# A two-layer graph network on one core: where five pieces of work stand, and which engine and queue they use

## The chip, the core and the metric

The kernel runs on one core of a Trainium2 chip. A core has five engines with a queue of instructions each: TensorE (PE in the profile, with PEld for its loads of weights), VectorE (DVE), ScalarE (ACT), GpSimd (POOL) and SyncE (SP). Each works through its queue in order and waits on semaphores for the others. Transfers are issued from the queues of SP, POOL and ScalarE and run on 16 DMA engines. The metric is the time of one execution on the device in microseconds, smaller being better; it is given as the median of several executions.

## The reference

x holds 128 graphs of 128 nodes with 256 features, adj their adjacency. Both layers begin with a normalization over the features and a relu, and add their result to x. Cut to what matters:

```python
# layer 0
h = relu(layernorm(x))
xc   = transpose(h)                                   # features by nodes
c    = bn2(conv17(relu(bn1(conv1(xc)))))              # 1x1, then 17 taps along the nodes
x_conv = transpose(relu(c + xc))
s    = h @ w_se.T + b_se                              # embedding of 3 numbers per node
A    = exp(-squared_distances(s)) * adj
x_nmp = A @ relu(h @ w_msg.T + b_msg)
r, z, n = GRU gates of (concat(x_conv, x_nmp), h)     # sigmoid, sigmoid, tanh
x = x + (1 - z) * n + z * h
# layer 1: only nodes 0 to 24 change
h = relu(layernorm(x))
for g, idx in enumerate(GROUPS):                      # five sets of 25, 9, 7, 6, 6 nodes
    a = normalized(adj[:, idx][:, :, idx] + I)
    o = relu(a @ relu(a @ h[:, idx] @ W1[g] + b1[g]) @ W2[g] + b2[g])
    fused[:, idx] += softmax(fusion_w)[g] * o
x = x + fused
```

Everything is float32.

## The kernel before

The graphs are taken in 32 groups of four (`q`). The 17-tap convolution is done by Fourier products: a forward transform of each half of a graph (80 points), one product per frequency, and an inverse transform. The 32 groups form two batches of 16 for this.

The program has these stages:

- **Stage A** (`stage_a`, one per group) loads x (`load_x`, four pieces on SP's queue, L360), takes the moments (`moments`: L267, L268, L269 on VectorE, then `rs` on POOL, L270), scales (`normalize`, L275), transposes (`ph`, L387), applies the relu into `hTa` (L389) and stores it to device memory (`hTd`, POOL, L392), multiplies with the 1x1 convolution (`pc`, L398), and transforms (`pf`, L409) into `X` (L415, L417). Four buffers hold x, two hold `hTa`.
- **`tap_weights`** runs beside stage A of the first batch. It loads the taps (`wt`), transforms them (`pw`, L451) through three staging buffers `ws`, and stores them (`wfd`, POOL, L463). At a certain step it calls `load_late`, which loads `wse` (L252) and the later part of the constants `cst` (L253) on SP's queue. At its end it opens the pools in which the neighbour stage works.
- **Stage B** (`stage_b`, once per batch) makes the 40 frequency products: `load_w` loads the transformed taps three steps ahead (`wf`, L488), `add` forms sums on POOL, PE makes `pa` and `pb` (L502), VectorE and ScalarE evacuate them into `y` (L524, L525), and POOL stores `y` to `yd` (L529).
- **`early`** (one per group) is the neighbour stage: it loads `hT` and `adj` (L540, L542), makes the embedding `pse` (L581), four scalings of it into `ef` (two on VectorE, L586, two on ScalarE, L589), their products `lr` (L592), the messages (`pm`, L601, and L604, L606), the distances `pd` (L614), exp times adjacency `aT` (L618, L619), and `px` (L627), stored on POOL's queue (`xmd`).
- **`fold_gates`** loads the gate weights and forms sums of them on POOL (L323); it runs in the second batch.
- **Stages N and C** load what the earlier ones stored and make the inverse transform (`pi`, L674), the gates (`p`, L709) and the new x (`po`, L855).
- **Layer 1** runs beside stage C: `setup_1` (loads, and the softmax of `fusion_w` with its product `s2w`, L895 to L907), `rows`, `prepare` and `block`, the last once per 16 graphs. A block ends with four quarters of four graphs, each with three steps: `turn` transposes (L1062, copied at L1066), `gather` multiplies with the adjacency (L1074, L1076, L1077), and `fuse` adds the groups together and onto x (L1083, L1085). Then four stores of x to `out` follow on POOL's queue (L1094).

The order of the instructions is fixed when the program is built. Each stage is a generator whose `yield a, b` says how much of PE's time its step takes and how long its result takes to come; `Lane` and `Order` interleave these programs on a planned clock. A batch runs its stage A with `beside` (taps, then neighbour groups) until stage A is done, then stage B with `beside`:

```python
begin = Lane([stage_a(q) for q in range(bat * BQ, (bat + 1) * BQ)], ahead=3)
order.run(begin, beside, *[gates] * bat, until=begin)
...
order.run(products, beside, *[gates] * bat, until=products)
```

So a step that is moved changes what the planner puts after it. Buffers of the on-chip memory are given out by pools; where a pool takes over the place of a closed one, a tile waits for the tiles that lay there before.

Of the kernel before, what the change touches and what calls it, by code (L numbers as in the profile page):

```python
# [9 lines left out]
FP = mybir.dt.float32  # L10
AF = mybir.ActivationFunctionType
# [196 lines left out]
def kernel(ctx: ExitStack, tc: tile.TileContext, x, adj, consts, vecs, w_se, conv1_w,  # L208
# [41 lines left out]
    def load_late():  # L250

        nc.sync.dma_start(out=wse, in_=w_se.rearrange("(k p) o -> p k o", p=P))  # L252
        nc.sync.dma_start(out=cst[:, CFIRST:], in_=consts[:, CFIRST:])  # L253

    scl, sft = {}, {}
# [84 lines left out]


# [26 lines left out]
    def stage_a(q):  # L368
# [6 lines left out]
        if q not in MOM:  # L375
            MOM[q] = moments(XA[q], "a")
            yield 0.0, 3.0
            normalize(XA[q], XA[q], *MOM[q])
            yield 0.0, 2.0
# [56 lines left out]
    def tap_weights():  # L436

        yield 0.0, 16.0
        for n in range(4):
            for m in range(8):  # L440
                if m == (0 if n else 3) and n < 3:
                    load_taps(n + 1, nc.sync, nc.gpsimd)
                if (n, m) == (2, 4):
                    load_late()
                if m % 2 == 0:
                    ws = tw.tile([P, 4, 4, D], FP, tag="ws", name=f"ws{n}_{m}", bufs=3)
                pws = [(pgat if r < 3 else ptmp).tile([P, 2, D], FP, tag="gat" if r < 3 else "tmp",
                                                      name=f"pw{n}_{m}_{r}") for r in range(4)]
                for r in range(4):
                    rows = slice(32 * r, 32 * r + TAPS)  # L450
                    nc.tensor.matmul(pws[r][:F], c("tap")[rows], wts[n][rows, 2 * m:2 * m + 2],  # L451
                                     start=True, stop=True)
                i = m % 2 * 2
                for r in range(4):
                    if r < 2 or (r == 2 and m % 2):
                        nc.scalar.activation(ws[:F, r, i:i + 2], pws[r][:F], AF.Copy)
                    else:
                        nc.vector.tensor_copy(ws[:F, r, i:i + 2], pws[r][:F])
                yield 0.9, 2.2
                if m % 2:  # L460
                    for r in range(4):
                        i0 = 64 * r + 16 * n + 2 * (m - 1)
                        nc.gpsimd.dma_start(out=wfd[:, i0:i0 + 4], in_=ws[:F, r])  # L463
# [6 lines left out]
        LATE["io"] = near.enter_context(tc.tile_pool(name="io", bufs=2, reuse_waits="tile"))  # L470
        LATE["fr"] = near.enter_context(tc.tile_pool(name="fr", bufs=1, reuse_waits="tile"))
# [6 lines left out]
    def stage_b(bat):  # L478
# [29 lines left out]
        for f in range(NF + 1):  # L508
            if f + 3 <= NF:
                load_w(f + 3)  # L510
            if f < NF:
                add(f + 1)
            y = xf.tile([P, 2, D], FP, tag="y", name=f"y{bat}_{f}")
# [61 lines left out]
    def neighbours(q, hT, ad, xm):  # L575
# [8 lines left out]
        for i in range(4):  # L584
            if i % 2 == 0:
                nc.vector.tensor_scalar(ef[:, i], pse[:, :N], emb[:, i:i + 1], embb[:, i:i + 1],  # L586
                                        op0=ALU.mult, op1=ALU.add)
            else:
                nc.scalar.activation(ef[:, i], pse[:, :N], AF.Identity, scale=emb[:, i:i + 1],  # L589
                                     bias=embb[:, i:i + 1])  # L590
# [280 lines left out]
    def setup_1():  # L871
# [9 lines left out]
        fus = pool.tile([P, NG], FP, name="fus")  # L881
        nc.sync.dma_start(out=fus, in_=fusion_w.partition_broadcast(P))
# [10 lines left out]

        fmx = pool.tile([P, 1], FP, name="fmx")
        nc.vector.reduce_max(fmx, fus, axis=mybir.AxisListType.X)  # L895
        nc.vector.tensor_scalar(fus, fus, fmx, None, op0=ALU.subtract)  # L896
        nc.scalar.activation(fus, fus, AF.Exp)
        fsm = pool.tile([P, 1], FP, name="fsm")
        nc.vector.reduce_sum(fsm, fus, axis=mybir.AxisListType.X)
        nc.vector.reciprocal(fsm, fsm)  # L900
        nc.vector.tensor_scalar(fus, fus, fsm, None, op0=ALU.mult)
        nc.vector.tensor_mul(fus, fus, c("grp"))
        wrow = pool.tile([P, 1], FP, name="wrow")
        nc.vector.reduce_sum(wrow, fus, axis=mybir.AxisListType.X)
        s2w = S["s2w"] = pool.tile([P, 2 * WIDE], FP, name="s2w")
        nc.vector.tensor_scalar(s2w, c("s2"), wrow, None, op0=ALU.mult)
# [95 lines left out]
    def block(blk):  # L1002
        while not (blk in P_DONE and blk - 1 in B1_DONE):
            yield 0.0, 0.5
        pool, yz, b2row, s2w = S["pool"], S["yz"], S["b2row"], S["s2w"]
# [51 lines left out]
        def turn(q):  # L1057
# [7 lines left out]
            zt = zts[q] = pool.tile([P, 2, D], FP, tag="zt", name=f"zt{blk}_{q}", bufs=3)  # L1065
# [13 lines left out]
        def fuse(q):  # L1079
# [5 lines left out]
            nc.vector.tensor_add(x1[:, q], x1[:, q], pf)  # L1085

        for what, q in ((turn, 0), (turn, 1), (turn, 2), (gather, 0), (gather, 1), (fuse, 0),
                        (turn, 3), (gather, 2), (fuse, 1), (gather, 3), (fuse, 2), (fuse, 3)):
# [4 lines left out]
        for j in range(GB):  # L1093
            nc.gpsimd.dma_start(  # L1094
                out=out[blk * SB:(blk + 1) * SB, :WIDE].rearrange("(q j) n c -> j n q c", j=GB)[j],
                in_=x1[j * WIDE:(j + 1) * WIDE])
# [11 lines left out]
    gates = Lane([fold_gates()], weight=0.5)  # L1108
# [61 lines left out]
```

## Time and profile before

| | us |
|---|---|
| median of 3 executions | 2099.61 |
| lowest, highest | 2089.95, 2099.69 |
| the profiled execution: its own time | 2107.02 |
| the profiled execution: span from the first to the last instruction | 2105.2 |
| PE busy in the span | 2045.2 |
| DVE, ACT, POOL busy | 1181.8, 686.8, 725.5 |
| mean granted TensorE clock | 0.986 |

The stages of the profiled execution lie in time as follows: stage A of the first batch to about 178 us, stage B to 372, stage A of the second batch to about 535, its stage B to 706, then stages N and C with layer 1 beside them to about 2015, and the last block of layer 1 to the end.

A wait is written as engine, tile and line, an arrow, and who released it; then the sum, the count and the longest in us. A window's row gives the stretch and its length, the busy time of each engine with its count of instructions, the granted clock, the share of the DMA engines' time and the rate. A timeline's row gives start, length, engine, line, operation and tiles, and in brackets the idle time before and its releaser. Letters after an engine's name: a q (SPq, POOLq) is its sequencer, which issues and waits.

### The profile page before, as it was taken

The page shows a single profiled execution, that of the slowest core. Times are in us where ns is not written, and L with a number is a line of the kernel's source. Part 1 is how long each engine was busy: PE and PEld are TensorE (multiplying, and loading weights), DVE is VectorE, ACT ScalarE, POOL GpSimd, SP SyncE. Part 2 cuts the span into 40 slices and gives each one's busy share as a digit, 9 for nine tenths or more (in the row PEclk, how much of TensorE's full clock was granted, in tenths as well). Part 3 has the DMA queues.
Part 4 walks back from the last instruction along what each step waited for, and adds up shares of the span by engine and source line. Part 5 has one row for each costly group of instructions (what it writes and reads, how often), then busy time and mean ns, then how long its engine had stood idle before and what let it go on. Part 6 is the DMA issues. An engine that isn't in the chain of part 4 may idle for free.

```text
span 2105.2 us, 31050 instructions
## 1 busy us (share of the span) xinstructions
PE 2045.2 (97%) x11316; PEld 1657.3 (79%) x11316; DVE 1181.8 (56%) x2775; ACT 686.8 (33%) x1543; POOL 725.5 (34%) x902
## 2 busy tenths in 40 slices
PE   7978999999999999999999999999999999999998
PEld 5656888789888788787878877878787787878875
DVE  6754544786544455655654565565565655654642
ACT  4643222344222333323232232232233223223333
POOL 3432666232565222503322233224323323233230
PEclk9989999999999999999999999999999999999999
DMA  9977778744777634222323332323232333223121
GB/s 217 276 227 231 240 266 264 211 153 143 250 258 257 210 111 141 75 78 73 89 71 92 87 83 72 88 71 91 75 96 73 79 91 93 78 81 98 31 79 51
DMA packets 186870, 281.67 MB, mean 134 GB/s; under 512 B 20745, under 2 KB 139982, under 8 KB 186718
## 3 DMA queue, kind: packets, MB, share of 16 engines
q1 hardware_dynamic: 156270, 185.00, 31.0%
q0 software_dynamic: 30160, 94.46, 14.1%
q8 instruction: 90, 1.47, 0.3%
q14 instruction: 62, 0.51, 0.1%
q10 hardware_dynamic: 288, 0.22, 0.0%
HBM read 187.34 MB, written 92.27 MB: 133 GB/s over the span
## 4 chain that ended last, share of the span: by engine, by line
PE 91%; DMA 4%; DVE 2%; issue 1%; POOL 1%; ACT 0%; SPq 0%; POOLq 0%; DVEq 0%; ACTq 0%
PE p L709 41%; PE pa L502 7%; PE pm L601 5%; PE ph L1031 5%; PE pz L1040 5%; PE pc L398 4%; PE pb L502 3%; PE pi L674 3%; PE px L627 3%; PE pf L409 2%; PE pg L1074 1%; PE ph L387 1%; PE pc L688 1%; PE po L855 1%; DMA xa<-in_x 1%; PE py L1014 1%
## 5 line engine op out<-in xcount | busy, mean ns | idle before, releaser
L835 POOL TENSOR_TENSOR d<-hTc,r 128x512 f32<-128x512 f32 x64 | 81.3, 1271 | 370.9 <-ACT r L832 370.9
L502 PE MATMUL pa<-wf,X 128*128 128x256 f32 x640 | 152.5, 381 | 0.0
L864 POOL DMA_DIRECT2D out<-xt x128 | 71.9, 567 | 211.0 <-DVE xt L861 205.4
L525 DVE SCALAR_TENSOR_TENSOR y<-pa,kk 128x512 f32<-128x512 f32 x78 | 53.8, 690 | 147.0 <-ACT kk L524 147.0
L398 PE MATMUL pc<-c1w,hTa 128*128 128x256 f32 x512 | 125.4, 392 | 6.6 <-DVE X L415 4.3
L709 PE MATMUL p<-th,wrz 128*128 128x256 f32 x512 | 131.7, 380 | 0.0
L724 ACT ACTIVATE z<-z,brz 128x256 f32<-128x256 f32 x128 | 58.1, 501 | 225.5 <-DVE z L781 191.2
L709 PE MATMUL p<-tc,wrz 128*128 128x256 f32 x512 | 131.6, 380 | 0.0
L709 PE MATMUL p<-tm,wrz 128*128 128x256 f32 x512 | 131.5, 380 | 0.0
L502 PEld LDWEIGHTS pa<-wf,X 128*128 128x128 f32 x640 | 118.3, 190 | 16.2 <-issue 2.2
L601 PE MATMUL pm<-wmsg,hT 128*128 128x256 f32 x512 | 124.4, 389 | 0.0
L691 DVE SCALAR_TENSOR_TENSOR xc<-pc,s_bn,hTc 128x256 f32<-128x256 f32 x128 | 53.1, 478 | 118.3 <-PE pc L688 118.3
L398 PEld LDWEIGHTS pc<-c1w,hTa 128*128 128x128 f32 x512 | 96.0, 195 | 25.9 <-DVE X L415 4.5
L601 PEld LDWEIGHTS pm<-wmsg,hT 128*128 128x128 f32 x512 | 97.9, 194 | 16.7 <-issue 1.8
L1031 PE MATMUL ph<-yz,w 128*128 128x96 f32 (+3 forms) x640 | 109.2, 325 | 0.9 <-DVE yz L1016 0.9
L1033 ACT ACTIVATE hh<-ph,vec 128x96 f32<-128x96 f32 (+3 forms) x160 | 64.0, 402 | 134.2 <-PE ph L1031 124.7
L709 PEld LDWEIGHTS p<-tm,wrz 128*128 128x128 f32 x512 | 97.5, 190 | 13.0
L1040 PE MATMUL pz<-hh,w 128*128 128x96 f32 (+3 forms) x640 | 107.3, 322 | 0.0
L1031 PEld LDWEIGHTS ph<-yz,w 128*128 128x128 f32 x640 | 88.1, 193 | 21.9 <-issue 13.2
L709 PEld LDWEIGHTS p<-tc,wrz 128*128 128x128 f32 x512 | 95.2, 190 | 12.0 <-issue 0.5
L709 PEld LDWEIGHTS p<-th,wrz 128*128 128x128 f32 x512 | 94.9, 190 | 12.1 <-DVE fus L896 0.3
L709 PE MATMUL p<-hTc,wrz 128*128 128x256 f32 x384 | 103.9, 394 | 0.0
(204 smaller groups left out, 4562.0 us busy)
## 6 DMA issues: line engine op xcount, KB each, us to landing
wf<-wfd SPq DMA_DIRECT2D x160, 256.0 KB, 4.1
wfd<-ws POOLq DMA_DIRECT2D x64, 320.0 KB, 8.2
yd<-y POOLq DMA_DIRECT2D x80, 256.0 KB, 3.8
yt<-yd SPq DMA_DIRECT2D x64, 320.0 KB, 4.9
w<-in_W SPq DMA_DIRECT2D x40, 512.0 KB, 3.7
xa<-in_x SPq DMA_DIRECT2D x128, 128.0 KB, 5.2
hTd<-hTa POOLq DMA_DIRECT2D x32, 512.0 KB, 5.8
hT<-hTd SPq DMA_DIRECT2D x32, 512.0 KB
```

The lines of the kernel that those rows point to most:

```text
L398: nc.tensor.matmul(pc[:, i], hT[:, k, (2 * h + i) * N:(2 * h + i + 1) * N], c1w[:, k], start=(k == 0), stop=(k == 1))
L502: nc.tensor.matmul(ps, xk(k), WF[f][:, k, s], start=(k == 0), stop=(k == 1))
L601: nc.tensor.matmul(pm[:, i], hT[:, k, j * N:(j + 1) * N], LATE["wmsg"][:, k], start=(k == 0), stop=(k == 1))
L627: nc.tensor.matmul(px[:, dc, i], msgs[h][:, i, dc * P:(dc + 1) * P], aT[:, 2 * h + i], start=True, stop=True)
L674: nc.tensor.matmul(pi[b * 64:(b + 1) * 64], inv[:F], yt[:, b::2], start=True, stop=True)
L709: nc.tensor.matmul(ps[:, m], w[:, i, k, m * P:(m + 1) * P], factor(i, x, t), start=first and j == 0, stop=last and j == len(n) - 1, skip_g ...
L724: nc.scalar.activation(dst[:, m], src[:, m], AF.Sigmoid, bias=brz[:, b + m:b + m + 1])
L835: nc.gpsimd.tensor_sub(d, hT[:, dc], r[:, dc])
L864: nc.gpsimd.dma_start(out=out[q * GB + j, WIDE:].rearrange("(t n) c -> n t c", n=WIDE), in_=xt[j * WIDE:(j + 1) * WIDE, 1:4])
L1031: nc.tensor.matmul(ph, w1[:, k, m * P:(m + 1) * P], yz[:, k, :, o:o + n], start=(k == 0), stop=(k == 1))
L1033: nc.scalar.activation(hh[:, m], ph, AF.Relu, bias=v("b1", g * 4 + m))
L1040: nc.tensor.matmul(pz, w2[:, g, m, cc * P:(cc + 1) * P], hs[g][:, m], start=(m == 0), stop=(m == 3))
```

## The change

Five edits are made together.

1. The load of `fusion_w` (`fus`) moves from `setup_1` into `load_late`, and `load_late` is called at step (1, 3) of `tap_weights` instead of (2, 4).
2. The softmax of `fusion_w` moves from `setup_1` into a program of its own, `fold_fusion`, which follows `fold_gates` in the same lane; `fus` and `s2w` lie in the pool of constants.
3. Stage B of the first batch loads x of groups 16, 17 and 18 in its steps 33, 36 and 39 into a new pool `xe`, which is opened ahead of the pool `fr`; it takes the moments of group 16 in step 36 and scales it in step 38. In stage A, groups 17 and 18 wait 1 and 12 us of the planned clock before their moments.
4. All four scalings `ef` are made by ScalarE.
5. The last steps of a block stand in another order, with four buffers `zt` in place of three. Each quarter is stored as soon as it is fused: one store on POOL's queue for blocks 0 to 6; for block 7 four stores, on SP's queue, those of the last quarter in turn on SP's and ScalarE's.

```diff
     def load_late():
 
+        nc.sync.dma_start(out=fus, in_=fusion_w.partition_broadcast(P))
         nc.sync.dma_start(out=wse, in_=w_se.rearrange("(k p) o -> p k o", p=P))
         nc.sync.dma_start(out=cst[:, CFIRST:], in_=consts[:, CFIRST:])
 
+    fus = cp.tile([P, NG], FP, name="fus")
+    s2w = cp.tile([P, 2 * WIDE], FP, name="s2w")
...
+    def fold_fusion():
+
+        fmx = cp.tile([P, 1], FP, name="fmx")
+        nc.vector.reduce_max(fmx, fus, axis=mybir.AxisListType.X)
+        nc.vector.tensor_scalar(fus, fus, fmx, None, op0=ALU.subtract)
+        nc.scalar.activation(fus, fus, AF.Exp)
+        yield 0.0, 4.0
+        fsm = cp.tile([P, 1], FP, name="fsm")
+        nc.vector.reduce_sum(fsm, fus, axis=mybir.AxisListType.X)
+        nc.vector.reciprocal(fsm, fsm)
+        nc.vector.tensor_scalar(fus, fus, fsm, None, op0=ALU.mult)
+        yield 0.0, 4.0
+        nc.vector.tensor_mul(fus, fus, c("grp"))
+        wrow = cp.tile([P, 1], FP, name="wrow")
+        nc.vector.reduce_sum(wrow, fus, axis=mybir.AxisListType.X)
+        nc.vector.tensor_scalar(s2w, c("s2"), wrow, None, op0=ALU.mult)
+        yield 0.0, 0.0
...
         if q not in MOM:
+            if BQ < q < BQ + 3:
+                yield 0.0, 11.0 * (q - BQ) - 10.0
             MOM[q] = moments(XA[q], "a")
...
-                if (n, m) == (2, 4):
+                if (n, m) == (1, 3):
                     load_late()
...
         LATE["io"] = near.enter_context(tc.tile_pool(name="io", bufs=2, reuse_waits="tile"))
+        LATE["xe"] = near.enter_context(tc.tile_pool(name="xe", bufs=1, reuse_waits="tile"))
         LATE["fr"] = near.enter_context(tc.tile_pool(name="fr", bufs=1, reuse_waits="tile"))
...
             if f < NF:
                 add(f + 1)
+            if f >= NF - 6 and f % 3 == 0 and bat + 1 < NBAT:
+                n = (bat + 1) * BQ + (f - NF + 6) // 3
+                XA[n] = LATE["xe"].tile([P, 4, D], FP, name=f"xa{n}")
+                load_x(XA[n], n)
+            n = (bat + 1) * BQ
+            if f == NF - 3 and n in XA:
+                MOM[n] = moments(XA[n], "a")
+            if f == NF - 1 and n in XA:
+                normalize(XA[n], XA[n], *MOM[n])
...
         for i in range(4):
-            if i % 2 == 0:
-                nc.vector.tensor_scalar(ef[:, i], pse[:, :N], emb[:, i:i + 1], embb[:, i:i + 1],
-                                        op0=ALU.mult, op1=ALU.add)
-            else:
-                nc.scalar.activation(ef[:, i], pse[:, :N], AF.Identity, scale=emb[:, i:i + 1],
-                                     bias=embb[:, i:i + 1])
+            nc.scalar.activation(ef[:, i], pse[:, :N], AF.Identity, scale=emb[:, i:i + 1],
+                                 bias=embb[:, i:i + 1])
...
-            zt = zts[q] = pool.tile([P, 2, D], FP, tag="zt", name=f"zt{blk}_{q}", bufs=3)
+            zt = zts[q] = pool.tile([P, 2, D], FP, tag="zt", name=f"zt{blk}_{q}", bufs=4)
...
             nc.vector.tensor_add(x1[:, q], x1[:, q], pf)
-
-        for what, q in ((turn, 0), (turn, 1), (turn, 2), (gather, 0), (gather, 1), (fuse, 0),
-                        (turn, 3), (gather, 2), (fuse, 1), (gather, 3), (fuse, 2), (fuse, 3)):
+            b0 = blk * SB + q * GB
+            if blk < NBLK - 1:
+                nc.gpsimd.dma_start(out=out[b0:b0 + GB, :WIDE], in_=x1[:, q])
+                return
+            for j in range(GB):
+                eng = nc.scalar if q == QS - 1 and j % 2 else nc.sync
+                eng.dma_start(out=out[b0 + j, :WIDE], in_=x1[j * WIDE:(j + 1) * WIDE, q])
+
+        for what, q in ((turn, 0), (turn, 1), (turn, 2), (gather, 0), (turn, 3), (gather, 1),
+                        (gather, 2), (fuse, 0), (gather, 3), (fuse, 1), (fuse, 2), (fuse, 3)):
             what(q)
...
-        for j in range(GB):
-            nc.gpsimd.dma_start(
-                out=out[blk * SB:(blk + 1) * SB, :WIDE].rearrange("(q j) n c -> j n q c", j=GB)[j],
-                in_=x1[j * WIDE:(j + 1) * WIDE])
...
-    gates = Lane([fold_gates()], weight=0.5)
+    gates = Lane([fold_gates(), fold_fusion()], weight=0.5)
```

In `setup_1` the load of `fus` and the lines of the softmax, which are the same as those of `fold_fusion`, are taken out.

More of the change, by code (lines that the diff above doesn't have):

```diff
@@ L880, in setup_1 @@
         nc.sync.dma_start(out=b2s, in_=b2)
-        fus = pool.tile([P, NG], FP, name="fus")
-        nc.sync.dma_start(out=fus, in_=fusion_w.partition_broadcast(P))
         for n in range(2):
@@ L892, in setup_1 @@
             yield 0.0, 4.0
[L894 to L906, printed above, removed]
         b2row = S["b2row"] = pool.tile([P, D], FP, name="b2row")
@@ L1004, in block @@
             yield 0.0, 0.5
-        pool, yz, b2row, s2w = S["pool"], S["yz"], S["b2row"], S["s2w"]
+        pool, yz, b2row = S["pool"], S["yz"], S["b2row"]
         w2, ac, r4 = S["w2"], S["ac"][blk % 2], S["r4"][blk % 2]
```

## The prediction

> **What bounds the kernel now.** First the busy shares and the slices:
>
> ```profile
> PE 2045.2 (97%) x11316; PEld 1657.3 (79%) x11316; DVE 1181.8 (56%) x2775; ACT 686.8 (33%) x1543; POOL 725.5 (34%) x902
> ...
> PE   7978999999999999999999999999999999999998
> ...
> PEclk9989999999999999999999999999999999999999
> DMA  9977778744777634222323332323232333223121
> ```
>
> TensorE (PE) is busy for 97%, so a change can win only where PE is idle or slowed. The table of windows (us; PE busy, PEld, DVE, ACT, POOL, granted clock, DMA share, GB/s) says where:
>
> ```profile
> 100.00:150.00 50.00, 39.03 (x205) 25.00 (x198) 26.87 (x71) 21.13 (x45) 19.41 (x29) 0.83 0.80 235
> ...
> 175.00:205.00 30.00, 19.86 (x135) 15.96 (x133) 9.25 (x20) 8.02 (x21) 0.54 (x1) 0.83 0.69 215
> 205.00:370.00 165.00, 164.77 (x1001) 142.88 (x1002) 80.25 (x138) 40.39 (x109) 102.11 (x126) 1.00 0.79 258
> 370.00:450.00 80.00, 72.03 (x457) 61.50 (x456) 61.19 (x163) 30.45 (x71) 25.21 (x26) 0.96 0.64 189
> ...
> 725.00:2015.00 1290.00, 1286.05 (x6600) 1038.99 (x6600) 740.61 (x1725) 397.08 (x867) 380.39 (x447) 0.99 0.30 84
> ```
>
> Idle PE: 11.0 us at 100 to 150, 10.1 at 175 to 205, 8.0 at 370 to 450 (second batch's start), 4 in 1290 of the last phase. The clock loses 50x0.17 = 8.5, 30x0.17 = 5.1 and 80x0.04 = 3.2 us. PE's waits at 90 to 140, then at 370 to 450:
>
> ```profile
> PE pw L451 <- DVE X L415: 6.7, 1, 6.7
> PE pc L398 <- DVE X L415: 4.3, 1, 4.3
> ```
> ```profile
> PE pc L398 <- ACT ef L589: 2.3, 1, 2.3
> PE pf L409 <- ACT ef L589: 1.8, 1, 1.8
> PE pd L614 <- DVE msg L604: 1.3, 1, 1.3
> ```
>
> The first pair is not VectorE's doing. SP's timeline and the chain of waits (start, length) show a late load:
>
> ```profile
> 94.43 9.94 SPq L360 DMA_DIRECT2D xa<-in_x  x4
> 104.42 1.04 SPq L252 DMA_DIRECT2D wse<-in_w_se  x1
> 105.50 0.67 SPq L253 DMA_DIRECT2D cst<-in_consts  x1
> 109.08 28.83 SPq L360 DMA_DIRECT2D xa<-in_x  x16
> ```
> ```profile
> 114.36 20.09 DMA xa<-in_x
> ```
>
> The four x pieces of group 12 begin at 109.1, behind wse and cst, and take 20 us to land (114.4+20.1 = 134.5). The group's moments (L267) stand in VectorE's queue until then, the copy into X (L415) stands behind them, and PE runs dry. So the gap that the list puts down to X is a DMA's.
>
> [...] eight pc matmuls take 3.71 us at 139.4, after the 6.7 us gap, against 1.73 elsewhere; so an idle microsecond costs more than itself. [...] Here ef alternates VectorE and ScalarE on one bank, and the timeline at 375.6 shows them strictly in turn, each waiting for the other. [...] four L275 at 424.4 take 5.04 us beside the gate-weight sums (L323), 1.37 at 405.9; the 2.3 us wait is just behind. [...]
>
> **The change, part by part.**
>
> *Constants, older place.* Three SP issues (fus 2.5 KB, new here; wse 67 KB; cst 461.5 KB) move from between x of groups 11 and 12 (104 us) to between groups 8 and 9, at about 62 us. In SP's waits, later issues stand until earlier transfers are done: group 11 is done at 115.3, wse at 122.5, cst at 124.8, group 12 at 134.5. So up to 124.8-115.3 = 9.5 us of this queue's service lay ahead of group 12. Gain: at most the 6.7 us gap and 5.0 of clock (125 to 150 ran at 0.80), 11.7; I take 6, about half: the loads of groups 13 to 15 stand close behind, and with a DMA share of 1.03 up to 100 us the stores on POOL's queue will take part of the freed service. Cost: groups 9 and 10 come up to 9.5 us later. Group 10 lands at 82.3 and its moments are at 98.4; group 9 lands about 77 (between its issue at 65.5 and group 10's) and is used at 88.3, spare 11; SP then idles until 89.7, when PE releases the next taps' buffer. The cover is that spare; without it PE idles at 85 to 95. Past this point the stores on POOL's queue pass 0.53 MB more: at 265 GB/s 2 us, of which the hTa wait at 80.3 (1.1 us) might give 2 to PE. Bounds -11.7 to +4.
>
> *Second batch's begin ahead.* x of groups 16, 17, 18 (12 SP issues, 12x0.43 = 5.2 us) is loaded into a new pool in steps 33, 36, 39 of the first batch's products. Moments of 16 (4x(0.39+0.18)+0.17 = 2.5 us of VectorE, one 1.0 us rs on POOL) go before step 36, four scalings (4x0.41) at step 38. All this moves out of 376 to 386, just ahead of which and in which PE waits for msg behind it (1.3 us); x of 17 and 18 no longer waits for the products' buffers, and transposes of 16 are ready for PE as the products end. In place of it: SP's wf loads queue behind up to 2.2 us per group, the load having three steps (12 us) of lead against 4.1 to land; 1.5 MB goes into a stretch at 79% DMA share (1.5 MB/258 GB/s = 6 us of transfer, spread over 27). POOL's rs stands before the y store and the next step's sums, and VectorE's st before y. Behind each waits PE through three gat banks. Hidden by the lead: cost 0.5, bounds 0 and 4.
>
> *ef on ScalarE.* 2x0.41 us of VectorE per group becomes 2x0.457 of ScalarE (64 in all: -26 us, +29 us; ScalarE is at 33%). The chain pse to lr goes from 1.9 us (375.6 to 377.5) to about 4x0.43 = 1.7, and no longer stands behind VectorE's queue. Its in-order risk: hTa and h relus come 0.9 us later; nothing idles for them in 450 to 700.
>
> These two together have 7.6 us of gaps (372 to 443) and 3.2 of clock: I take 7 (bounds 2 and 10.8). What is late next: lr itself, still on VectorE ahead of pd.
>
> *Near pool shifted by the new tiles.* wmsg and bmsg no longer lie over the last staging tile; their 0.39+0.47 us of issue no longer stand ahead of hT at 181.3, inside the 9.1 us gap: -0.9, bounds 0 and -2.
>
> *Softmax moved.* Nine small VectorE and ScalarE instructions (2.5 us together) leave 850 to 853 for the second batch's phases; PE is full in both. Zero, cover PE's own queue; 1 us if it stands before an ef or y. The planner shifts two neighbour groups into the last phase; that phase's opening gaps (2.9+0.8+0.3 us at 715 to 723) may close in part: -0.5, bounds -3 and +3.
>
> *Stores by quarters, block order.* Seven blocks keep four POOL issues (0.55 us each), now in quarters; each waits for its own L1085 add, ahead of the gate sums, while PE has 0.3% idle: zero. In the last block the chain
>
> ```profile
> 2098.18 0.42 DVE L1085 TENSOR_TENSOR x<-x,pfu 128x256 f32<-128x256 f32 x1 [1.09 <-PE pfu L1083]
> 2098.90 2.17 POOL L1094 DMA_DIRECT2D out<-x  x4 [35.87 <-DVE x L1085]
> ```
>
> shortens: fuse 1 and 2 fill the wait for the last relu, so the last add ends at about 2097.4 instead of 2098.6. But SP now issues 14 pieces at 0.47 us from the first add at 2094.5, to 2101.0, about when POOL ended (2101.1). POOL's drain until 2104.5 goes: -1.5, bounds -2.7 and +0.3.
>
> Sum: -6+0.5-7-0.9-0.5-1.5 = **-15.4 us**. The profiled execution took 2107.02 (span 2105.2 and 1.8 around), 7.4 above the median of three, 2099.61; where the clock windows fall varies that much. From its own time that gives 2091.6. The measured time is a median, so I subtract from the median: 2084.2, and since a run with less clock loss has a little less to win, about **2085**. The clock alone is worth some 4 us either way.
>
> **Rivals.**
> *Both sides of the first gap close*: constants -11.7, the rest as summed: 2099.6-11.7-9.4 = 2078. For: the slots at 122.5 and 124.8. Against: DMA share near 1 until 125.
> *Only the second batch gains*: the transfer is hidden anyway, since stores take the freed service: 2099.6-9.4 = 2090.
> *The begin ahead moves the stall*: in stage B x lands as late as in the opening (15 us median there), 3 past its lead, with 3 of clock; then 2085+6 = 2091.
> *Slower*: the moved constants starve group 9. Price: if 512 pieces (128 fus, 256 wse, 128 cst) are served like the 512 of one x load, 20 us (the chain's 20.09). Decides from 11 us. Then group 9 comes 9 late, group 10's 20 eat its 16 and the later loads follow: +20 idle and 2.5 of clock, not regained if stores fill the later place: 2099.6+22.5-9.4 = 2113. Against: only 9.5 us for wse and cst later on.
>
> **How the numbers follow.** Forecast 0.42 (2078 to 2093), both sides 0.16, only second batch 0.22, stall moved 0.08, slower 0.12. 0.5% (10.5 us; about what a measurement tells) puts the line at 2089.1: faster 0.35+0.16+0.05 = 0.56; slower (above 2110.1) 0.09; the rest 0.35. The range 2071 to 2103 leaves out most of the last case and the bounds' far end.
>
> **What would show it.** Right: no 6.7 us PE wait for X near 131, granted clock above 0.9 in 125 to 150; no PE wait for ef at 395 or 429, windows 370 to 450 above 77 busy; SP's stores, not POOL's, ending the chain. Wrong: waits of st for xa at 85 to 100, PE idle in 340 to 370 behind y, or the same PE gaps with another releaser.

## The result, and the profile after

| | median, us | runs, us | ratio to before (95%) |
|---|---|---|---|
| before | 2096.74 | 2089.95 to 2099.69, five | |
| changed | 2074.16 | 2071.19 to 2078.33, five | 0.9908 (0.9883 to 0.9933) |
| changed, again beside the experiments | 2074.47 | 2069.94 to 2079.54, six | 0.9914 (0.9892 to 0.9936) |

The change takes off 0.9%, 18 to 19 us by the ratio (the two medians of the table are 22.6 us apart); the forecast was 2085 out of 2099.61, or 14.6 less. Below, too, gains in us are worked out from the ratio, which is not exactly that of the two medians. In the three sets of experiments below, the kernel before ran 95 more times: medians 2094.08, 2091.98 and 2093.19, single runs from 2086.6 to 2106.3. So its profiled execution, 2107.02, stands at the slow end of its own spread. That turned out to matter more than anything else in the prediction.

The page of the changed kernel: busy shares, then the slices.

```profile
PE 2032.3 (98%) x11316; PEld 1649.4 (80%) x11316; DVE 1161.9 (56%) x2711; ACT 712.7 (34%) x1611; POOL 730.1 (35%) x898
...
PE   7998999999999999999999999999999999999998
...
PEclk9999999999999999899999999999999999999999
DMA  9997788545777444223323232322232332323121
```

The same windows as before the change (us; PE busy, PEld, DVE, ACT, POOL, granted clock, DMA share, GB/s):

```profile
100.00:150.00 50.00, 50.00 (x310) 33.82 (x303) 38.17 (x100) 32.59 (x69) 26.15 (x38) 1.00 0.93 286
175.00:205.00 30.00, 28.69 (x212) 24.50 (x213) 15.67 (x29) 11.64 (x34) 8.94 (x12) 1.00 0.75 236
...
370.00:450.00 80.00, 76.98 (x496) 68.99 (x495) 65.12 (x174) 38.44 (x87) 28.35 (x29) 0.98 0.50 157
725.00:2015.00 1290.00, 1284.01 (x6670) 1035.42 (x6670) 734.31 (x1705) 404.75 (x881) 398.87 (x471) 0.99 0.30 85
```

PE was busy for 39.0 of the 50 us from 100 to 150 and is now busy throughout, at full clock. From 370 to 450 it is busy for 77.0 where it was 72.0. PE's waits over the whole run, the largest ones behind the start:

```profile
PE pse L614 <- DMA hT<-hTd: 6.6, 1, 6.6
PE p L738 <- DVE r L854: 2.8, 2, 2.5
PE px L656 <- DVE aT L648: 2.3, 3, 1.0
PE p L738 <- ACT u L772: 1.6, 1, 1.6
```

No wait for X stands there any more, and none for ef. The first pse, the first work on the neighbours, waits for hT of group 0; behind the start it is the one large gap left. In the tail the timeline ends like this (start, length):

```profile
2061.66 6.67 SPq L1105 DMA_DIRECT2D out<-x  x14
...
2064.32 0.42 DVE L1098 TENSOR_TENSOR x<-x,pfu 128x256 f32<-128x256 f32 x1 [0.74 <-PE pfu L1096]
2064.77 0.83 ACTq L1105 DMA_DIRECT2D out<-x  x2
```

SP's stores are the last work of the run, as foreseen, and not POOL's. Read alone, this pair of traces says: the opening gained 19 us (first pse at 187.2, now 167.9), all through the moved constants, and the second batch the rest. The experiments do not bear out the first half of that.

### The profile page after: what moved, and what is told of

The parts are those of the page before. It is cut to its first block, busy times and chain, and to the rows that moved or that the text cites. A ratio compares the mean times of both kernels' runs of the same rounds, so it can differ in the third digit from the quotient of the medians.

```text
span 2070.6 us, 31082 instructions
## 1 busy us (share of the span) xinstructions
PE 2032.3 (98%) x11316; PEld 1649.4 (80%) x11316; DVE 1161.9 (56%) x2711; ACT 712.7 (34%) x1611; POOL 730.1 (35%) x898
## 4 chain that ended last, share of the span: by engine, by line
PE 93%; DVE 2%; DMA 2%; POOL 1%; issue 1%; ACT 1%; SPq 0%; DVEq 0%; POOLq 0%; ACTq 0%
PE p L738 42%; PE pa L526 7%; PE pm L630 5%; PE ph L1044 5%; PE pz L1053 5%; PE pc L421 4%; PE pb L526 3%; PE pi L703 3%; PE pf L432 3%; PE px L656 3%; PE pg L1087 2%; PE po L884 1%; PE pc L717 1%; PE pw L474 1%; PE ph L410 1%; PE py L1027 1%
## 5 line engine op out<-in xcount | busy, mean ns | idle before, releaser
L1044 PEld LDWEIGHTS ph<-yz,w 128*128 128x128 f32 x640 | 86.7, 190 | 21.0 <-issue 15.4
```

Source lines behind the costliest of these rows:

```text
L1044: nc.tensor.matmul(ph, w1[:, k, m * P:(m + 1) * P], yz[:, k, :, o:o + n], start=(k == 0), stop=(k == 1))
```

## The experiments

The change has five parts: constants, begin ahead (with the new pool), ef, tail (stores by quarters, order of the block, a fourth zt) and softmax. Each was put into the kernel before by itself.

**e1: the constants alone**

```
-                if (n, m) == (2, 4):
+                if (n, m) == (1, 3):
                     load_late()
```

> The kernel before, with only the place of the two late loads wse and cst changed: right behind x of group 9's load (about 62 us) and not between x of groups 11 and 12. TensorE's order stays word for word that of before. Theory A (the place of these loads alone makes the whole gain of the opening): about 19 us less, 2078; both early gaps of TensorE (4.3 at 114, 6.7 at 131) gone, granted clock 1.00 from 100 to 150, the first pse at 168 to 171 where it was at 187. Rival A2 (the prediction's size; the other half of the opening's gain is from the near pool's new tiles, which take wmsg and bmsg off the last staging tile): 6 us less, 2091, first pse near 181. Rival A3 (it comes from where the clock's windows fell in the one profile): no more than 3 us less, 2094, the gaps stay.

Measured: 2094.85 against 2094.08, ratio 0.9998 (0.9982 to 1.0013). Nothing, the size of rival A3, but not its gaps that stay: the trace shows what A asked for, PE busy 50.00 of 50 from 100 to 150, clock 1.00. PE's waits from 20 to 205:

```profile
PE pse L581 <- DMA hT<-hTd: 13.3, 1, 13.3
PE pf L409 <- ACT hTa L389: 1.3, 1, 1.3
```

The X gaps are gone, and the gap for hT is 13.3 us where it was 9.1. PE reached the first pse 15 us sooner than in the profile of before (163.4 against 178.1), but the last store of the staging tiles landed at 169.5 and hT behind it.

**e3 and e4** are also repeats of the opening, for up to the first pse they are the kernel before, constants late and all. PE's waits from 20 to 205, e3 and then e4:

```profile
PE pse L581 <- DMA hT<-hTd: 10.1, 1, 10.1
PE px L623 <- DVE aT L615: 1.0, 1, 1.0
```
```profile
PE pse L581 <- DMA hT<-hTd: 8.8, 1, 8.8
PE pc L398 <- DVE X L415: 1.4, 1, 1.4
```

The same program, and the 11 us of X gaps are 0 and 1.4. In the eight profiles with the constants late PE's waits for X come to 11.0, 4.1, 0, 1.4, 2.8, 0.7, 3.7 and 8.9 us; in five with them early (e9, which leaves loads out, apart) to 0, 0, 0, 3.6 and 2.0.

Two loads are mixed in these sums. The first wait of VectorE is for x of group 11, which is issued at 93 to 95 us, ahead of the late place of the constants; it comes in all eight profiles with the constants late (0.7 to 10.0 us) and in three of the five with them early (up to 4.6). The second is for group 12, the one behind the constants, on which the prediction built its first term. Group 12 in the profile before, then in e6 (below), and group 11 in e12 (below):

```profile
134.58 0.43 DVE L267 BATCH_NORM_STATS2 st<-xa 128x6 f32<-128x256 f32 x1 [9.59 <-DMA xa<-in_x]
```
```profile
125.32 0.43 DVE L270 BATCH_NORM_STATS2 st<-xa 128x6 f32<-128x256 f32 x1 [3.35 <-DMA xa<-in_x]
```
```profile
118.99 0.43 DVE L270 BATCH_NORM_STATS2 st<-xa 128x6 f32<-128x256 f32 x1 [9.96 <-DMA xa<-in_x]
```

VectorE's wait for group 12 was 9.6 us in the profile before, 0.6 to 3.4 in four of the other seven with the constants late, and did not show in the rest, nor in any with them early. PE itself stood for it 6.7 us in the profile before and 0.4 at most in the others. So the place of the constants has an effect on group 12, but its size in the profile before is an accident of one run.

**e3: ef on ScalarE alone**

```
-            if i % 2 == 0:
-                nc.vector.tensor_scalar(ef[:, i], pse[:, :N], emb[:, i:i + 1], embb[:, i:i + 1],
-                                        op0=ALU.mult, op1=ALU.add)
-            else:
-                nc.scalar.activation(ef[:, i], pse[:, :N], AF.Identity, scale=emb[:, i:i + 1],
-                                     bias=embb[:, i:i + 1])
+            nc.scalar.activation(ef[:, i], pse[:, :N], AF.Identity, scale=emb[:, i:i + 1],
+                                 bias=embb[:, i:i + 1])
```

> The kernel before, with only the four scalings ef of each group put on ScalarE. TensorE's order stays. Theory C (it removes the two waits of TensorE for ef, 2.3 and 1.8 us, and with them the 3 us of clock that 370 to 450 loses; the msg wait stays): 3 to 6 us less, about 2092. Rival C2 (ef was only the last of several releasers: VectorE's queue with the moments and normalisations behind it holds lr and X just as long): under 2 us less, 2095 to 2097, the gaps with another name. In both the rest of the run from 450 on is unchanged, as ScalarE is a third busy.

Measured: 2086.61, ratio 0.9957 (0.9940 to 0.9974), 9 us. This is theory C's mechanism at more than its size (3 to 6 us). PE's waits from 352 to 450, first e1 (ef as before), then e3:

```profile
PE pc L398 <- ACT ef L589: 2.3, 1, 2.3
PE pf L409 <- ACT ef L589: 1.8, 1, 1.8
PE pd L614 <- DVE msg L604: 1.3, 1, 1.3
```
```profile
PE pd L610 <- DVE msg L600: 1.0, 1, 1.0
PE px L623 <- DVE aT L615: 0.9, 1, 0.9
```

Both waits for ef are gone, nothing of their size takes their place, and the granted clock of this window goes from 0.98 to 1.00. From the last product of the first batch to the first pi the trace takes 346.1 us, where the four profiles of this stretch as it was (before, e1, e4, e12) have 351 to 354.

**e2: the begin ahead alone** (pool xe; loads, moments and scaling in stage_b; the two pauses)

```
+            if f >= NF - 6 and f % 3 == 0 and bat + 1 < NBAT:
+                n = (bat + 1) * BQ + (f - NF + 6) // 3
+                XA[n] = LATE["xe"].tile([P, 4, D], FP, name=f"xa{n}")
+                load_x(XA[n], n)
...
```

> The kernel before, with only the second batch's begin ahead: the new pool xe, x of groups 16 to 18 loaded in the first batch's products, moments and scaling of group 16 there, and the two pauses ahead of the moments of 17 and 18. Constants late, ef still by turns on VectorE and ScalarE. It also changes the order in which TensorE meets the second batch's groups, neighbours and products. Theory B (it makes most of the second batch's 12 us by itself): 9 to 12 us less, 2085 to 2088; TensorE's idle time from 370 to 450 (shifted by nothing, since the opening stays) falls from 8 to under 4. Rival B2 (the embedding scalings make the gain, the load ahead is hidden anyway): under 3 us less, 2094 or more, with the waits for ef still there. Rival B3 (the loads ahead cost the first batch's products): gaps of PE behind y or wf in 330 to 370, total the same or above.

Measured: 2086.61, ratio 0.9959 (0.9942 to 0.9976), 8.6 us: just under the 9 to 12 of theory B. From 200 to 369 one gap of PE is over 0.3 us, 0.6 ahead of a pd, so the loads ahead cost the products nothing (B3 falls). PE's waits from 352 to 450:

```profile
PE pc L400 <- ACT hTa L391: 2.5, 1, 2.5
PE pd L626 <- DVE h L403: 1.2, 1, 1.2
PE pf L411 <- ACT ef L601: 0.9, 1, 0.9
```

Idle PE there is 7.0 of 98 us, and in e1 7.5: the idle time fell little, and theory B's sign (from 8 to under 4 between 370 and 450) did not come, with 5.8. What changed is its shape and the order: one of the two ef waits is left, the clock is 1.00, and part of the neighbours' work (16 pse, 8 pm, 8 pd and 16 px, an estimated 10.3 us by their durations) now runs in the last phase. The run also has the shifted near pool of the new tiles; none has that pool without the loads ahead.

**e10: begin ahead and ef together**

> The kernel before, with the begin ahead and the scalings ef on ScalarE together; constants late, tail and softmax as before. Alone they measured -0.41% and -0.43%. Theory G (they take different parts of the second batch's start, so they add up): -0.75 to -0.85%, 2075 to 2078. Rival G2 (both take the same waits at 370 to 450): -0.5 to -0.6%, 2081 to 2084. In the trace from the last product of the first batch to TensorE's end: 1728 before, 1720 with ef, 1723 with the begin ahead; G wants 1715 to 1716, G2 1719 or more.

Measured: 2079.78, ratio 0.9931 (0.9913 to 0.9948), 14.4 us, between G and G2. The trace takes 1719.4 us from the last product of the first batch to PE's end, which is G2's sign. With the 10.3 us of moved work added back, the second batch takes 341.5 us where it took 352, with the begin ahead alone 345.1 and with ef alone 346.1: gains of 10.5, 7 and 6. So the two overlap by 2 to 3 us in the second batch. From 352 to 450 no wait for ef or msg of over 0.5 us is left:

```profile
PE pd L622 <- DVE h L403: 1.2, 1, 1.2
PE ph L389 <- DVE aT L627: 0.9, 1, 0.9
```

**e4: the tail alone** (the part of the diff from zt to the new order)

> The kernel before, with only the last layer's part: block 0 to 6 store by quarters, block 7 in 16 pieces on SP and ScalarE, the new order of turn, gather and fuse, four zt tiles. Theory D (the prediction's): the last add about 1 us earlier, and 1.5 us from the drain of POOL's stores, 1 to 3 us less, 2094 to 2096: beside the run-to-run spread of 0.25% not to be seen in the median, but in the trace as the time from the last gate product to the end: 90.4 us before, 88.2 in the changed kernel. Rival D2 (quarters on POOL's queue get in the way of the gate sums there): TensorE idles in 800 to 2000 behind z or d, some us more, above 2099.

Measured: 2089.38, ratio 0.9978 (0.9963 to 0.9992), 4.6 us. From the last gate product to the end the trace has 87.9 us (before 90.4, changed 88.2): the 2.5 us of theory D, of which 1.4 lie ahead of the last add. No gap behind z or d shows, so D2 falls by its own sign; but PE now has two waits for u, a tile of the gates like r and v, of 1.8 and 1.6 us, at 984 and 1056, which neither before nor e1 has. All the same the last phase is 6 us shorter, and that is the granted clock: its stretches at half clock come to some 17 us in before and to under 2 in e4. One of them, some 7 us between 1034 and 1065, stands in before, e1, e3 and e12 alike and is missing in e4; from 850 to 2015 the granted clock is 0.99 in those four and 1.00 in e4. Before, then e4 (the columns as in the windows above):

```profile
1040.00:1080.00 40.00, 39.81 (x181) 31.42 (x181) 24.58 (x60) 9.82 (x21) 19.06 (x28) 0.91 0.32 87
```
```profile
1030.00:1080.00 50.00, 48.36 (x229) 39.04 (x228) 37.54 (x87) 13.58 (x31) 17.53 (x23) 1.00 0.24 64
```

So the 4.6 us of the median may well be more than the tail alone; which part of the edit the clock answers to was not tried.

**e12: the softmax alone**

```
-    gates = Lane([fold_gates()], weight=0.5)
+    gates = Lane([fold_gates(), fold_fusion()], weight=0.5)
```

> The kernel before, with only the softmax of the fusion weights moved from the last phase's set-up into the lane of the gate weights, and fus loaded with wse and cst at their later place. Theory I (the prediction's): nothing, within 2 us of the kernel before; TensorE's order stays. Rival I2 (the set-up of the last phase is short of VectorE at 850, so taking nine small instructions from there helps): the gap of 1.8 us for r near 865 goes, with its clock windows: 2 to 5 us less.

Measured: 2096.10, ratio 1.0017 (1.0003 to 1.0031). No gain, and more likely some 3 us of loss than theory I's nothing (within 2 us); the wait of PE for r near 875 stays at 1.8 us, so I2 falls here. The profile has 8.9 us of X gap in the opening, for group 11; whether the small pieces of fus, issued behind that load, make the X gaps likelier was not measured.

Beside the begin ahead it may be otherwise. In e10, where work of the neighbours has moved to this place, PE's waits from 700 to 900 are:

```profile
PE p L717 <- DVE r L825: 1.9, 1, 1.9
PE p L717 <- DVE r L833: 1.8, 2, 1.5
PE p L717 <- DVE v L819: 1.5, 1, 1.5
```

and the softmax stands just ahead of them on VectorE:

```profile
844.00 0.16 DVE L907 TENSOR_REDUCE fsm<-fus 128x1 f32<-128x5 f32 x1 [1.83 <-ACT fus L905]
```

That step waits 1.83 us in order for ScalarE's exponential. In the changed kernel the wait for v is gone, and those for r come to 3.5 us and not 3.7 in the same window. That is read from two traces and not tried alone.

**e5 and e6: the changed kernel again, and with its constants late**

```
-                if (n, m) == (1, 3):
+                if (n, m) == (2, 4):
                     load_late()
```

> The changed kernel once more, for a second profile of it and more runs in the company of the others. Sum of the parts measured alone (constants -0.02%, begin ahead -0.41%, ef -0.43%, tail -0.22%): -1.08%, so 2071 to 2072 if the parts add up and the moved softmax is nothing. If they overlap (begin ahead and ef both work on the second batch's start): 2074 to 2078, a ratio of 0.991 or more.

> The changed kernel, with fus, wse and cst loaded at the later place again (between x of groups 11 and 12), all else as changed. Theory E (the opening ends when the last tap-weight stores on POOL's queue are through, because the first hT of the neighbours lies over the last staging tile; what the constants delay is regained in that wait): the same as the changed kernel within 0.2%, 2070 to 2076; a gap of TensorE for X near 115 to 131, and a shorter one for hT near 165. Rival E2 (with wmsg and bmsg off the last staging tile the place of the constants is worth the 6 us predicted, or more): 2080 or more.

Measured: e5 2074.47, 0.9914 (0.9892 to 0.9936), e6 2080.01, 0.9934 (0.9913 to 0.9955). The ratios are 0.20% apart with overlapping intervals, the medians 5.5 us. The ten runs of e6 spread from 2073.0 to 2089.4, and its median is outside E's 2070 to 2076 and just at E2's 2080. E's sign fails as well: e6's gap for hT is 7.5 us, no shorter than the 6.6 and 6.3 of the changed kernel, and its first pse comes at 175.1 and not at 167.9, so what the late x cost was not regained. This pair leans to E2, e1 and the next pair don't. The second trace of the changed kernel repeats the first in the opening to 0.1 us.

**e7 and e8: hT of group 0 off the last staging tile**

```
-        LATE["io"] = near.enter_context(tc.tile_pool(name="io", bufs=2, reuse_waits="tile"))
-        LATE["xe"] = near.enter_context(tc.tile_pool(name="xe", bufs=1, reuse_waits="tile"))
         LATE["fr"] = near.enter_context(tc.tile_pool(name="fr", bufs=1, reuse_waits="tile"))
+        LATE["io"] = near.enter_context(tc.tile_pool(name="io", bufs=2, reuse_waits="tile"))
+        LATE["xe"] = near.enter_context(tc.tile_pool(name="xe", bufs=1, reuse_waits="tile"))
```

> The changed kernel, with the three pools of near opened in the order fr, io, xe and not io, xe, fr: hT of group 0 moves from under the last staging tile ws (free at its last store, 164.1 in the profile) to under the one before (157.1). No instruction moves on any engine. Theory E (the opening waits for the last staging tile's stores): hT of group 0 is issued at 158 and not at 164, the gap of TensorE before the first pse falls from 6.6 to 0 to 3, with it the half-clock window behind it: 4 to 9 us less than the changed kernel, 2064 to 2069. Rival E3 (the DMA engines are the bound there, so hT's landing stays; or the wait goes over to wf, whose loads stand behind all stores anyway): no gain, 2072 to 2075, a gap before pa in its place.

> The order of pools fr, io, xe and the constants at the later place. Theory E: with the wait for the last staging tile gone, what is late ahead of it is no longer regained, so now the constants' place counts: 4 to 10 us slower than the kernel with the pools in this order and constants early, about 2072 to 2076. Rival E4 (the x gaps seen in one profile of before are chance and the place is worth nothing in any surroundings): the same within 0.2% as the one with constants early.

Measured: e7 2078.34, 0.9931 (0.9911 to 0.9952); e8 2076.64, 0.9922 (0.9903 to 0.9942). No gain, so E's expectation for e7 failed; that is E3's outcome, though 2078.34 is above its 2072 to 2075 and no gap before pa took the place. SP's waits of e7 from 150 to 176:

```profile
SPq L573 <- DMA hT<-hTd: 3.5, 1, 3.5
SPq L573 <- DMA wfd<-ws: 3.1, 1, 3.1
```

hT is issued at 164.3 and not at the 158 hoped for (PE stood 3.6 us for X in this profile), while the last tile's stores are still on their way (the last lands at 171.8), so the two are under way together: the first pse starts 10.2 us after hT's issue, where the changed kernel, which waits for the stores, needs 3.6. In e8 it is issued at 161.7, 9.3 us earlier than in e6, and the first pse comes 3.5 us earlier, at 171.6. So most of an earlier issue went into a longer landing, and no gain in the total can be told. Between e7 and e8 the constants' place makes -0.1%: rival E4 held here.

**e9: fewer bytes**

```
+            if q in (9, 11, 13, 15):
+                XA[q] = XA[q - 1]
+                return
             XA[q] = LATE["ab"].tile([P, 4, D], FP, tag="xa", name=f"xa{q}", bufs=4)
             load_x(XA[q], q)
```

> The changed kernel, with x of groups 9, 11, 13 and 15 not loaded: the tile of the group ahead is used again, so the output isn't the reference's. Moments, scalings and all of TensorE's work stay; 16 SP issues and 2.1 MB go out of an opening that moves 39 MB from 20 to 160 us with the DMA engines at 9 tenths in every slice. Theory F (the bytes of the opening set its end, and each load that comes earlier makes others later): 2.1 MB at 279 GB/s, 7.5 us earlier for the last store and for hT of group 0: first pse at 160 to 163 where it was at 167.8, the gap for hT from 6.5 to under 2, and 5 to 9 us less than the changed kernel in all, 2065 to 2069. Rival F2 (the stores wait for VectorE's and ScalarE's copies, or for POOL's issue): less than 2 us, first pse at 166 or later. Rival F3 (single loads that come late set it): the X gap near 114 doesn't show, the hT gap stays 6 us.

Measured: 2073.72, 0.9904 (0.9887 to 0.9921): the changed kernel's time, and the first pse at 170.2. F falls. The windows of e9:

```profile
100.00:130.00 30.00, 30.00 (x187) 20.00 (x180) 23.62 (x64) 19.65 (x42) 15.89 (x23) 1.00 0.97 293
130.00:160.00 30.00, 30.00 (x188) 22.25 (x187) 20.70 (x57) 18.47 (x40) 15.79 (x23) 1.00 0.76 225
```

PE is full there, as in the changed kernel, and with fewer bytes it can be no fuller: it comes to the first pse at 161.3 in both. The last staging store is issued at 155.8 in both, since PE's own work sets when the tile is filled. It lands 8 to 10 us later, and hT 4 us behind it. So in a run in which no x comes late, the opening is PE's work plus one latency at its end; late loads come on top in others.

**e11: a pause ahead of the first neighbours**

```
+        if q == 0:
+            yield 0.0, 4.0
         yield from neighbours(q, hT, ad, xm)
```

> The changed kernel, with a pause of 4 us in the planner ahead of the first neighbour group, so that the last four pf of group 15 (2.6 us) stand ahead of the first pse in TensorE's queue, in the gap for hT. The planner also moves the first pa one neighbour group forward. Theory H: 2 to 4 us less than the changed kernel (2.6 us of work goes into a gap of 6.5[...]), 2070 to 2072. Rival H2: the first products now wait for wf, whose loads cannot begin before TensorE frees their buffers and the stores are through: the same gap at pa, 2074 to 2077.

Measured: 2073.85, 0.9903 (0.9883 to 0.9923), not to be told from the changed kernel. The gap for hT falls to 3.8 us as H says, and no gap before pa takes its place (H2 falls). But the clock still halves for about 7 us there: 0.51 from 171 to 178, as from 166 to 173 in the changed kernel. The profile also has 2.0 us of X gap, and 2.5 us more in the second batch. A gain could not be shown.

## Why the prediction was right or wrong

Stretches of TensorE's time in the traces, us. "Moved" is the 10.3 us of neighbours' work that the begin ahead puts into the last phase, taken back here.

| kernel | first batch, to its last product | second batch | last phase to PE's end | to the end of the span |
|---|---|---|---|---|
| before | 369.2 | 352.5 | 1376.4 | 7.1 |
| e1, constants | 359.6 | 351.2 | 1375.9 | 7.1 |
| e3, ef | 354.6 | 346.1 | 1374.0 | 7.1 |
| e4, tail | 355.5 | 353.6 | 1370.4 | 6.0 |
| e10, ahead and ef | 355.0 | 341.5 | 1377.9 | 7.0 |
| changed | 350.4 | 341.3 | 1372.6 | 6.3 |
| changed again (e5) | 350.3 | 339.8 | 1371.7 | 6.3 |

The direction and the range were right. The sum, -15.4 against 18 to 19 measured, was near for partly wrong reasons, and in that the prediction was lucky: one term rested on an accident, and others were too small by about as much. The measured 2074 lies below the forecast's own case (2078 to 2093) and nearest to the rival "both sides of the first gap close" (2078), but e1, which closes that gap, gains nothing. The begin ahead with ef (14.4) and the tail (4.6), measured without the rest, make 19.0 together.

*Constants, -6: wrong.* Measured alone -0.4 us, with an interval of -3.8 to +2.7. (That is wse and cst; in the changed kernel fus goes with them.) The step that failed is the first: to read the 4.3 and 6.7 us gaps of one profile as standing costs of the kernel. Its arithmetic (9.5 us of queue service, half of it to be had) rested on a landing that repeats of the same opening don't show, and the 4.3 us gap is for group 11, ahead of the constants. The bound of 11.7 also counts some time twice: from 131 to 138 PE was busy for 0.55 of 7 us at a granted clock of 0.66, so about 2 of its 5.0 us of clock lie inside the 6.7 us gap. The prediction noted that its profile was 7.4 us above the median and put this down to clock windows; it should have asked which gaps those 7.4 us were. The sign it named for this step, no 6.7 us wait near 131 and a granted clock above 0.9 from 125 to 150, came true in the changed kernel (1.00 from 100 to 150), but also in e1, which gained nothing, and in e3, where the constants are late. The rival "only the second batch gains" had this part right. Whether the place is worth a few us beside the other parts stays open: the X gaps of the profiles and the pair e5 and e6 (5.5 us between the medians) lean that way, e1 and the pair e7 and e8 don't.

*Near pool, -0.9: too small.* The issue of wmsg and bmsg was all that was priced. The row that shows the rest is hT's landing. SP in e4, where the old pools still stand:

```profile
166.01 0.39 SPq L474 DMA_DIRECT2D wmsg<-in_w_msg  x1
166.44 0.47 SPq L475 DMA_DIRECT2D bmsg<-in_b_msg  x1
167.02 0.37 SPq L540 DMA_DIRECT2D hT<-hTd  x1
```

and in the changed kernel:

```profile
157.39 0.39 SPq L498 DMA_DIRECT2D wmsg<-in_w_msg  x1
157.83 1.99 SPq L499 DMA_DIRECT2D bmsg<-in_b_msg  x1
164.23 0.34 SPq L573 DMA_DIRECT2D hT<-hTd  x1
```

From hT's issue to the first pse it takes 5.8 to 6.8 us in the five profiles with the old pools and 3.6 to 4.3 in the five with the shifted ones (pools in the changed kernel's order, e9 and e11 apart). The 384 KB of wmsg and bmsg no longer go just ahead of hT through the DMA engines. That is about 2.2 us beside the 0.9 of issue, some 3 in all; that these bytes are the reason is read from the traces, no run moves wmsg and bmsg alone. PE's gap for hT falls accordingly, from 8.8 to 13.3 in the one five to 6.0 to 7.5 in the other, and this is what is left of the opening's gain.

*Begin ahead and ef, -6.5 together: right in the waits that go, mis-sized.* The second batch gained 10.5 us, near the bound (10.8) and not the value taken (7), and the last phase gave about 1.5 back. Over the whole second batch PE's idle time went from 12.4 us before to 4.6 in e10, and the time at half clock from 6.8 to 3.4: the two parts take different waits. Part of the idle time that went lies outside the stretch from 372 to 443 in which the prediction looked. With the near pool's 3 us, which come with the new tiles, the second batch and the last phase account for about 12 of the 14.4 that the pair measures. Its cover held: no PE idle behind y or wf, and no cost of the 12 SP issues. What made VectorE and ScalarE take ef in turn, and L275 take 5.04 us beside the sums of L323, was not shown.

*Softmax, 0:* alone it measured between +0.6 and +6.5, a small loss that the prediction put at nothing; in the whole change it is not told apart.

*Tail, -1.5 within -2.7 to +0.3:* the trace has 2.5 in e4 and 2.2 in the changed kernel, at the far end. (The time from the last gate product to the end is 1.6 us longer in profiles with a half-clock stretch there: 89.8 in e5, with e1 and e3 at 92.0.) The last add came 1.4 earlier (worked out: 1.2); the drain went from 7.1 to 6.3 us behind PE's end. "Zero" for the seven earlier blocks left out that the new order moves PE's waits and the clock in the last phase, as e4 shows (under 2 us at half clock for some 17).

*The slower case* (group 9 starved by the constants): the first waits for st for xa at 85 to 100 came in none of the six profiles with the constants early; in e7 and e11 a wait of st for xa ends at 114.1 and 113.2 (4.6 and 3.1 us), but for group 11, as in the kernels with the constants late.

## What to carry to other kernels

A gap in one profile is a price only if it is there in the next one: where the profiled run is slower than the median, find the gaps that make the difference before building a term on them, and see for each which transfer it waits for. A sign that was foreseen and is seen proves a step only if it is absent without that step. And where a transfer is taken from just ahead of an urgent one, ask for its transfer time and not its issue time alone: here some 3 us in place of 0.9.

## What had not been expected of the hardware

The opening of one and the same program (before, e3, e4) reached its first pse between 171.7 and 187.2 us, with 0 to 11 us of waits for X. From the last product of the first batch to PE's end, before, e1 and e12, which differ there by the softmax alone, stay within 1727 to 1730. So the spread of 2086 to 2106 between single runs should come mostly from the opening. Its DMA row (40 slices of the window from 20 to 160 us, the changed kernel) shows what is special there:

```profile
DMA  9999998999999999999999999999999898279989
```

From issue to landing a piece of x took 10.7 us there (the median, at a DMA share of 0.99), and 2.6 from 372 to 540 (at 0.55). The load that came late was the same in most profiles, x of group 11, but it came between 110 and 119 us.

In e7 and e8 hT was issued without waiting for the last stores, and took 10.2 and 10.0 us from issue to the first pse, against 3.6 to 4.3 behind them. Most of an earlier issue was lost again: 5.8 of 9.3 us between e6 and e8.

The granted clock does not always follow PE's gaps. In the profile before it was 0.91 from 1040 to 1080 with PE busy for 39.81 of 40 us, and the same came in e1, e3 and e12; e4, which has a gap of 1.6 us there, kept 1.00. From 380 to 390 it was 0.83 with PE busy for 9.06 of 10. In the same profile it also halved in the gaps of 4.3, 6.7 and 9.1 us of the opening and stayed at 0.50 behind them, to about 123, 143 and 191 us; that is where the prediction read that an idle microsecond costs more than itself. The two stretches above have no such gap ahead of them: the last one is 1.3 us, up to 380.9, for the half clock from 382 to 386, and from 1040 to 1058, where the other begins, none is over 0.2. What set the clock in these was not shown.
